# Two seams and a tail of a four-layer graph network: weights made one stage earlier, smaller loads, and a separate closing of the last run

## The chip, the cores and the metric

The kernel runs on one core of a Trainium2 chip. The metric is the device time of one execution in microseconds (us). Before the change three runs gave 1075.41, 1076.99 and 1079.09 us; the median is 1076.99.

The engines are TensorE (PE in the profile, with its weight loads as PEld), VectorE (DVE), ScalarE (ACT), GpSimd (POOL) and SyncE (SP), which here issues most transfers.

## The reference

The input is a table `x` of 2708 rows of 128 numbers and a 2708 x 2708 adjacency matrix `adj`, symmetric in its pattern, with about 17 non-zero weights in a row. Four layers follow each other. Each takes `h = relu(layernorm(x))`, and adds its result to `x`:

- layer 0: `adj.T @ h`, divided by the column sums of `adj`;
- layer 1: for each edge a message `gelu(s[i] + d[j] + b)`, summed with the edge's weight, then an update with a gelu and a layer norm;
- layer 2: `msg = relu((adj @ h) @ W_msg.T + b)`, then a GRU cell with `msg` as input and `h` as state;
- layer 3: graph attention with two heads `k`.

Layers 2 and 3 are the ones that the change touches. Layer 3 is, for each head:

```
z     = ln(h, g1, b1);           hk = z @ ff0_w[k].T
e     = leaky_relu(s_src[:, None] + s_dst[None, :])     # from hk and attn_w
atten = softmax(where(adj > 0 or i == j, e, -9e15))
att   = ln(atten @ hk + h, g2, b2)
result += elu(att @ ff1_w[k].T) / 2
```

## The kernel before, in words

**Tiles.** The 2708 rows are `NT` = 22 row tiles of 128 (the last has 20). Layer 0 leaves the transposed adjacency in HBM as `adjT`, tile by tile. Layers 0 and 1 end at about 621 us. The change begins there.

**Layer 2, groups.** The output columns are taken in six groups of four row tiles (512 columns; the last has two tiles, 148 columns). For each group, TensorE sums `h.T @ adjT` over all 22 row tiles into one accumulator, `p_agg` (L1088). The `adjT` tiles come in pieces of `PIECE` = 5 row tiles through a pool `a2` of three buffers; SP issues the load (L1076). Each piece is also turned into a byte mask "greater than zero" for layer 3: VectorE does all tiles but the last of a piece in one instruction (L1080), GpSimd the last (L1083). A buffer is free for the next load when both masks and TensorE's products are through.

**Layer 2, closing a group.** `finish_chunk` is a Python generator with the GRU of one group, and then what layer 3 needs of it: the norm of `x` to `h3`, a second norm to `z`, its transpose `p_z`, the product with the weights `p_hv`, and from that `hv` (the rows to be averaged), `lift` and `row` (exponentials of the scores). The generator yields with a number, and is resumed while the next group's products are written.

**Order of work.** Inside this stage the order of instructions is the order of the Python code. A hand-kept clock decides when a generator is resumed: every piece of TensorE work calls `spend(units)`, and `advance()` resumes each generator in `following` whose time has come. A unit is about one 512-column product. So `spend` and `yield` move no data; they place instructions in the queues. Each engine runs its queue in that order.

**Layer 3, runs.** Columns are taken in four runs, `RUNS` = tiles 0 to 2, 3 to 10, 11 to 18, 19 to 21. For each of 22 row tiles and 2 heads there is one unit: VectorE makes the weights `wt = max(row, lift) * mask` (L917), and TensorE multiplies them with `hv` into accumulators `att` (L949), one matmul per column tile. `products` makes weights a number `ahead` of the products: 2 for run 0, which still overlaps the closing of the last two groups of layer 2, and 3 for the others. Run 0 takes its weight buffers from a pool `l3v` of 4, the others from a pool of 5. A tile can be weighed when `finish_chunk` has put it in `ready`; `advance()` is called until it is.

**Closing a run.** When a run's products are done, `evacuate` copies its sums out of the accumulators, and `close` handles two tiles at a time while the next run's products go on: four rows `att_s` on VectorE (L1012), their statistics (L118 and L119, then L120), a power on GpSimd for the inverse deviation (L121) with one Newton step on VectorE (`factors`, L127 to L131), scaling on ScalarE (L137), transposes `p_aT` (L1023), `z4T` on ScalarE, the product `p_o` (L1032), the elu (`el`, `po` on ScalarE, `less` on GpSimd, `y` on VectorE, L1040 to L1050) and the store. `close_run` starts the closings `apart` = 9 units after each other. The last run has no following run; `in_place` lets `close` read the accumulators themselves, with 2 units between its two closings.

Of the kernel before, what the change touches and what calls it, by code (L numbers as in the profile page):

```python
# [20 lines left out]
F32 = mybir.dt.float32  # L21
BF16 = mybir.dt.bfloat16
AF = mybir.ActivationFunctionType
ALU = mybir.AluOpType
# [6 lines left out]
P = 128  # L31
N = 2708
D = 128
# [3 lines left out]
CH = 512  # L37
# [10 lines left out]
GROUPS = [(t, min(4, NT - t)) for t in range(0, NT, 4)]  # L48
# [3 lines left out]
def size(t):  # L52
    return min(P, N - t * P)
# [7 lines left out]
def listed_layers(ctx: ExitStack, tc: tile.TileContext, x, adj, w, out, flag):  # L61
    nc = tc.nc
# [10 lines left out]
    xs = const.tile([P, NT, D], F32, name="xs")  # L73
# [12 lines left out]
    ident = const.tile([P, P], F32, name="ident")  # L86
# [794 lines left out]
    nc.gpsimd.memset(score[:, NT - 1, :], 0.0)  # L881
    ident_8 = l3.tile([P, P], U8, name="ident_8")
    nc.vector.tensor_copy(ident_8, ident)
    PIECE = 5
    RUNS = ((0, 3), (3, 8), (11, 8), (19, 3))
    MOST = 8
    accs = ctx.enter_context(tc.tile_pool(name="l23p", bufs=1, space=PSUM))
# [5 lines left out]
    def follow(steps):  # L893
        following.append([steps, clock[0]])

    def spend(units):
        clock[0] += units

    def advance():

        for f in list(following):
            while f[1] <= clock[0]:
                wait = next(f[0], None)
                if wait is None:
                    following.remove(f)
                    break
                f[1] = clock[0] + wait

    ready = set()
# [10 lines left out]
        )  # L920
        return wt

    def products(run, numbers, pool, ahead, before=None):

        banks = None
        wts = []
        units = 2 * NT
        touched = set()
        for u in range(units + ahead):
            if u < units:  # L930
                while u // 2 not in ready:
                    spend(0.5)
                    advance()
                wts.append(weigh(run, u, pool))
            v = u - ahead
            if v < 0:
                continue
            if v == 0:
                if before:
                    before()  # L940
                banks = banks_of(run, numbers)
            r0, rn = run
            j, k = divmod(v, 2)
            kj = size(j)
            wt = wts[v]
            for q in range(rn):
                m = size(r0 + q)
                s = k * rn + q
                nc.tensor.matmul(  # L949
                    banks[s // 3][0:m, s % 3, :], wt[0:kj, q * P : q * P + m], hv[0:kj, j, k, :],  # L950
                    start=(v < 2 and s // 3 not in touched), stop=(j == NT - 1), skip_group_check=True,
                )
                touched.add(s // 3)
            spend(0.29 * rn)
            advance()
        return banks
# [4 lines left out]
            for b in numbers[0 : (2 * run[1] + 2) // 3]  # L961
        ]

    def in_place(run, banks):

        r0, rn = run
        sums = [banks[s // 3][:, s % 3, :] for s in range(2 * rn)]
        inv3 = out_pool.tile([P, 2 * MOST], F32, name="inv3")
        for k in range(2):
            for q0, q1 in ((0, rn - 1), (rn - 1, rn)):  # L970
                m, s = size(r0 + q1 - 1), k * rn
                if q1 > q0:
                    nc.vector.reciprocal(
                        inv3[0:m, s + q0 : s + q1], banks[s // 3][0:m, (s + q0) % 3 : (s + q1 - 1) % 3 + 1, D]
                    )
        return sums, inv3, False

    def evacuate(run, banks):

        r0, rn = run  # L980
        res = out_pool.tile([P, 2 * MOST, D + 1], F32, name="res")
        inv3 = out_pool.tile([P, 2 * MOST], F32, name="inv3")
        tails = (rn - 1, 2 * rn - 1) if size(r0 + rn - 1) < P else ()
        for s in tails:
            nc.gpsimd.memset(res[:, s, :], 1.0)
        s = 0
        while s < 2 * rn:
            k = min(3 - s % 3, 2 * rn - s)
            m = P
            if s in tails:  # L990
                k, m = 1, TAIL
            elif s + k - 1 in tails:
                k -= 1
            copy = nc.vector.tensor_copy if s // 3 % 3 == 2 else nc.scalar.copy
            copy(res[0:m, s : s + k, :], banks[s // 3][0:m, s % 3 : s % 3 + k, :])
            s += k
        nc.vector.reciprocal(inv3[:, 0 : 2 * rn], res[:, 0 : 2 * rn, D])
        return [res[:, s, :] for s in range(2 * rn)], inv3, True

    def close(run, sums, first):  # L1000

        res, inv3, whole = sums
        k0 = min(2, run[1] - first)
        t0 = run[0] + first
        n = 2 * k0
        att = out_pool.tile([P, 4, D], F32, name="att_s")
        for s in range(n):
            i = s % 2 * run[1] + first + s // 2
            m = P if whole else size(t0 + s // 2)
            if m < P:  # L1010
                nc.gpsimd.memset(att[:, s, :], 0.0)
            nc.vector.scalar_tensor_tensor(  # L1012
                att[0:m, s, :], res[i][0:m, 0:D], inv3[0:m, i : i + 1], h3[0:m, t0 + s // 2, :],
                op0=ALU.mult, op1=ALU.add,
            )
        rows = tiles_of(att, 0, n)
# [36 lines left out]
        for q in range(k0):  # L1053
            m, i = size(t0 + q), (t0 + q) * P
            nc.sync.dma_start(out[i : i + m, :], y[0:m, q, :])

    def close_run(run, sums, apart=9):

        for first in range(0, run[1], 2):
            follow(close(run, sums, first))  # L1060
            yield apart

    with (
        tc.tile_pool(name="l2a", bufs=3) as apool,
        tc.tile_pool(name="l2g", bufs=1) as pool,
        tc.tile_pool(name="l2z", bufs=2) as zpool,
        tc.tile_pool(name="l3v", bufs=4) as vpool,
        tc.manual_schedule(),
    ):
        def aggregate(t0, k0, pa, j0):  # L1070
# [23 lines left out]
        def finish_chunk(t0, k0, pa):  # L1094
# [23 lines left out]
            for k in range(2):  # L1118
                nc.tensor.matmul(prz[k][:, 0:n], W_hhT[:, k * D : (k + 1) * D], hc[:, 0:n], start=True, stop=False)

            gate = pool.tile([D, 2, CH], F32, name="gate")
            for k in range(2):
                nc.tensor.matmul(prz[k][:, 0:n], W_ihT[:, k * D : (k + 1) * D], msg[:, 0:n], start=False, stop=True)
                nc.scalar.activation(gate[:, k, 0:n], prz[k][:, 0:n], AF.Tanh, bias=gate_b[:, k : k + 1], scale=0.5)
            nc.tensor.matmul(pi[:, 0:n], W_ihT[:, 2 * D : 3 * D], msg[:, 0:n], start=True, stop=True)
            spend(7 * u)
            nn = pool.tile([D, CH], F32, tag="t2", name="nn")
            nc.vector.scalar_tensor_tensor(
                nn[:, 0:n], gate[:, 0, 0:n], 1.0, half_n[:, 0:n], op0=ALU.add, op1=ALU.mult
# [68 lines left out]
            for k in range(2):  # L1198
# [2 lines left out]
                    passed[k * k0 : (k + 1) * k0, :].rearrange("t i -> (t i)")[0:n].partition_broadcast(P),  # L1201
                )

        for g, (t0, k0) in enumerate(GROUPS):
            pa = accs.tile([P, CH], F32, tag=f"acc{g % 2}", name="p_agg")
            for j0 in range(0, NT, PIECE):
                aggregate(t0, k0, pa, j0)
            if t0 == 0:
                late_weights()
            follow(finish_chunk(t0, k0, pa))  # L1210
            advance()
        last = RUNS[0]
        banks = products(last, (0, 1), vpool, 2)

    out_pool = ctx.enter_context(tc.tile_pool(name="l3o", bufs=2))

# [8 lines left out]
    with tc.tile_pool(name="l3w", bufs=5) as wpool, tc.manual_schedule():  # L1225
        for run, numbers in zip(RUNS[1:], ((2, 3, 4, 5, 0, 1), (2, 3, 4, 5, 0, 1), (2, 3))):

            def work_off(last=last, banks=banks):
                follow(close_run(last, evacuate(last, banks)))

            banks = products(run, numbers, wpool, 3, work_off)
            last = run
        follow(close_run(last, in_place(last, banks), 2))
        while following:
            spend(1)
            advance()


@with_exitstack
# [459 lines left out]
```

## Time and profile before

The profiled execution took 1077.95 us, and its span is 1076.2 us.

| what | us |
|---|---|
| median of the runs | 1076.99 |
| profiled execution / its span | 1077.95 / 1076.2 |
| TensorE busy / VectorE busy | 950.2 (88%) / 824.4 (77%) |
| layer 2 aggregation, first matmul to last group's end | 627.4 to 781.9 |
| run 0, first matmul to last | 784.7 to 830.1 |
| run 3 ends, first reciprocal of its closing | 1053.7 |
| last `y` ready / span ends | 1070.4 / 1076.2 |

Engines are idle and busy together; a share over the whole span hides which stage is bound by what. A group's row gives what the group's instructions took together, the mean of one, and the idle time of the engine just before them with what ended it. A stretch's row gives busy us and number of instructions per engine, then the granted TensorE clock (1.00 is full), the share of the DMA engines and GB/s. A line of the waits gives us in total, number, and the longest. A timeline line gives start, length, engine, line and operation, and in brackets the idle time before it and what ended it.

### The profile page before, as it was taken

Reading aid. Unit: us, or ns where it says so; the run is one execution under the profiler, and the core shown is the slowest. Engines: PE = TensorE matmul, PEld = TensorE weight load, DVE = VectorE, ACT = ScalarE, POOL = GpSimd, SP = SyncE. Lnnn points to the kernel's source line nnn. Section 1 sums busy time; section 2 is a strip of 40 time slices with the busy share of each in tenths; the row PEclk is TensorE's granted clock in tenths of the full one; section 3 lists DMA queues with packets and bytes.
Section 4 is the critical chain, followed back from the end, with each engine's and each line's share of the span. In section 5 each row is a group of like instructions: output and inputs, shape, how many; then the busy total and the mean of one; then the engine's idle time right before and its main releaser. Section 6 shows DMA issues by size and latency. Waiting matters only on the chain. (4 is left out here: it accounts for less than half of the span.)

```text
span 1076.2 us, 21996 instructions
## 1 busy us (share of the span) xinstructions
PE 950.2 (88%) x7950; PEld 756.6 (70%) x7950; DVE 824.4 (77%) x2856; ACT 516.5 (48%) x1431; POOL 398.0 (37%) x476
## 2 busy tenths in 40 slices
PE   5798889854699999999999979999978999999993
PEld 2454455433599999899998934444578999999762
DVE  7999999658577888887878265666578977997673
ACT  7777778444666566666576522333321200320142
POOL 3311112013686556666765253434410300440132
PEclk9999999755799999999999979999989999999996
DMA  9888897221133333223222065666300000000000
GB/s 367 312 308 291 311 344 257 57 72 55 54 124 103 118 115 112 83 85 108 85 89 75 29 215 199 206 215 211 106 21 26 7 3 1 6 16 1 1 16 14
DMA packets 60625, 129.67 MB, mean 120 GB/s; under 512 B 11160, under 2 KB 23828, under 8 KB 57798
## 3 DMA queue, kind: packets, MB, share of 16 engines
q1 hardware_dynamic: 58690, 125.38, 33.7%
q10 hardware_dynamic: 1816, 2.80, 0.8%
q8 instruction: 64, 1.05, 0.4%
q14 instruction: 55, 0.45, 0.1%
HBM read 81.55 MB, written 30.87 MB: 104 GB/s over the span
## 5 line engine op out<-in xcount | busy, mean ns | idle before, releaser
L949 PE MATMUL att<-hv,wt 128*128 128x129 f32 (+2 forms) x1936 | 243.8, 283 | 8.8 <-DVE wt L917 8.8
L949 PEld LDWEIGHTS att<-hv,wt 128*128 128x128 f32 (+2 forms) x1936 | 224.7, 192 | 25.7 <-DVE wt L917 10.2
L917 DVE SCALAR_TENSOR_TENSOR wt<-row,lift,mask 128x1024 f32<-128x1024 f32 (+5 forms) x176 | 160.2, 939 | 35.1 <-PE att L949 35.1
L530 POOL TENSOR_SCALAR put<-mine,value 128x128 f32<-128x128 bf16 x176 | 149.6, 866 | 70.3 <-DVE mine L427 68.0
L606 PE MATMUL p_m<-s,sel 128*128 128x128 bf16 x1452 | 161.6, 220 | 5.4 <-ACT g L618 5.4
L610 PE MATMUL p_m<-d,cols 124*128 124x128 bf16 (+1 forms) x1452 | 161.8, 220 | 1.4 <-DVE cols L560 1.3
L121 POOL TENSOR_TENSOR n_r<-n_r,minus_half 128x4 f32<-128x4 f32 (+1 forms) x31 | 46.1, 1486 | 292.4 <-DVE n_r L120 286.8
L631 PE MATMUL agg<-put,g 128*128 128x128 f32 (+1 forms) x968 | 135.9, 281 | 0.0
L296 PE MATMUL acc<-a,hs 128*128 128x512 f32 (+2 forms) x264 | 119.8, 563 | 11.1 <-ACT hs L137 11.1
L308 PEld LDWEIGHTS p_T<-ident,a 128*128 128x128 f32 x484 | 61.3, 147 | 85.7 <-issue 38.4
L631 PEld LDWEIGHTS agg<-put,g 128*128 128x128 f32 x968 | 118.2, 192 | 0.0
L1088 PE MATMUL p_agg<-a,hs 128*128 128x512 f32 (+2 forms) x264 | 109.4, 557 | 7.5 <-DMA a<-adjT 7.5
L606 PEld LDWEIGHTS <-sel 128*128 128x128 bf16 x1452 | 104.3, 98 | 10.8 <-issue 7.0
L308 PE MATMUL p_T<-ident,a 128*128 128x128 f32 x484 | 84.3, 295 | 30.9 <-ACT aT L312 23.5
L284 DVE FIND_INDEX8 col<-val,a 128x8 uint16<-128x124 f32 (+1 forms) x400 | 109.2, 290 | 0.0
L610 PEld LDWEIGHTS <-cols 124*128 124x128 bf16 (+1 forms) x1452 | 102.6, 98 | 1.9 <-DVE cols L560 1.9
L618 ACT ACTIVATE g<-p_m 128x512 f32<-128x512 f32 x132 | 73.0, 553 | 63.5 <-PE p_m L610 63.5
L538 ACT ACTIVATE put<-mine,value 128x128 f32<-128x128 bf16 x308 | 100.5, 391 | 0.0
L312 ACT ACTIVATE aT<-p_T 128x512 f32<-128x512 f32 (+2 forms) x132 | 71.1, 541 | 52.8 <-ACT aT L312 27.6
L282 DVE MAX8 val<-a 128x8 f32<-128x124 f32 (+1 forms) x400 | 94.2, 282 | 2.1 <-DMA a<-in_adj 2.1
L1088 PEld LDWEIGHTS p_agg<-a,hs 128*128 128x128 f32 (+1 forms) x264 | 47.6, 194 | 55.9 <-issue 54.3
L296 PEld LDWEIGHTS acc<-a,hs 128*128 128x128 f32 (+1 forms) x264 | 44.6, 199 | 31.2 <-issue 19.9
(249 smaller groups left out, 1423.7 us busy)
## 6 DMA issues: line engine op xcount, KB each, us to landing
a<-in_adj SPq DMA_DIRECT2D x21, 1354.0 KB
adjT<-aT SPq DMA_DIRECT2D x105, 256.0 KB
a<-adjT SPq DMA_DIRECT2D x20, 1280.0 KB
spread<-passed SPq DMA_DIRECT2D x22, 704.0 KB
later<-sel SPq DMA_DIRECT2D x22, 616.0 KB
row<-own_d ACTq DMA_DIRECT2D x10, 256.0 KB
later<-sel SPq DMA_DIRECT2D x22, 82.5 KB
adjT<-aT SPq DMA_DIRECT2D x21, 74.0 KB
```

What stands on the lines that cost most here:

```text
L282: nc.vector.max(val[:, n, b, :], block(b))
L284: nc.vector.max_index(col[:, n, b, :], val[:, n, b, :], block(b))
L296: nc.tensor.matmul(accs[ci][:, 0:cw], h[0:m, n, :], sets[n // 4][0:m, n % 4, c : c + cw], start=(n == 0), stop=(n == NT - 1),)
L308: nc.tensor.transpose(p[0:k, q * P : q * P + m], sets[gi][0:m, q, j * P : j * P + k], ident[0:m, 0:m])
L530: nc.gpsimd.tensor_scalar(st["put", 0][:, b, :], st["mine"][:, b, :], st["value"][:, b : b + 1], None, ALU.mult)
L538: nc.scalar.activation(st["put", 1][:, b - HP, :], st["mine"][:, b, :], AF.Identity, scale=st["value"][:, b : b + 1])
L606: nc.tensor.matmul(p[:, b - b0, :], st["sel"][:, b, :], s3[:, q, t % 2, :], start=(q == 0), stop=False)
L610: nc.tensor.matmul(p[:, b - b0, :], st["cols"][0:kb, b, :], d3[0:kb, b, q, :], start=False, stop=(q == 2))
L631: nc.tensor.matmul(agg, g[:, b - 4 * k, :], put, start=(b == 0), stop=False)
L917: nc.vector.scalar_tensor_tensor(wt[0:kj, :], row[0:kj, k, c : c + n], lift[0:kj, j, k : k + 1], mask[0:kj, j, c : c + n], op0=ALU.max, op ...
L949: nc.tensor.matmul(banks[s // 3][0:m, s % 3, :], wt[0:kj, q * P : q * P + m], hv[0:kj, j, k, :], start=(v < 2 and s // 3 not in touched), ...
L1088: nc.tensor.matmul(pa[:, 0:n], h[0:k, j, :], a[0:k, j - j0, 0:n], start=(j == 0), stop=(j == NT - 1))
```

## The change

Four things change, all in layers 2 and 3.

1. Pieces have four row tiles instead of five: six loads per group (4, 4, 4, 4, 4, 2), and the `a2` buffers shrink by a fifth. The pool `l3v` grows from 4 to 8 buffers.
2. While group 4 is aggregated, `weigh_ahead` makes two weights of run 0 after each piece but the first, up to seven, where their tiles are ready. `products` gets them as `made`, and works run 0 with 7 ahead. For the last, small group `finish_chunk` spends and yields once more between its gate matmuls.
3. The closings of run 2 start 7 units apart instead of 9.
4. The last run is closed by `close_last`, straight-line code in place of two resumed generators: both parts' statistics first, rows scaled alternately on ScalarE and VectorE, `z4T` of the second part and `po` on VectorE, and `less` and the clearing of short rows done beforehand by `last_rows`. `in_place` goes, and with it the flag `whole`.

```diff
--- before.py
+++ after.py
@@ -881,7 +881,7 @@
     nc.gpsimd.memset(score[:, NT - 1, :], 0.0)
     ident_8 = l3.tile([P, P], U8, name="ident_8")
     nc.vector.tensor_copy(ident_8, ident)
-    PIECE = 5
+    PIECE = 4
     RUNS = ((0, 3), (3, 8), (11, 8), (19, 3))
     MOST = 8
     accs = ctx.enter_context(tc.tile_pool(name="l23p", bufs=1, space=PSUM))
@@ -920,14 +920,20 @@
         )
         return wt
 
-    def products(run, numbers, pool, ahead, before=None):
+    def weigh_ahead(run, wts, pool, most):
+
+        for u in range(len(wts), min(len(wts) + 2, most)):
+            if u // 2 in ready:
+                wts.append(weigh(run, u, pool))
+
+    def products(run, numbers, pool, ahead, before=None, made=()):
 
         banks = None
-        wts = []
+        wts = list(made)
         units = 2 * NT
         touched = set()
         for u in range(units + ahead):
-            if u < units:
+            if len(wts) <= u < units:
                 while u // 2 not in ready:
                     spend(0.5)
                     advance()
@@ -961,20 +967,6 @@
             for b in numbers[0 : (2 * run[1] + 2) // 3]
         ]
 
-    def in_place(run, banks):
...
     def evacuate(run, banks):
 
         r0, rn = run
@@ -995,22 +987,19 @@
             copy(res[0:m, s : s + k, :], banks[s // 3][0:m, s % 3 : s % 3 + k, :])
             s += k
         nc.vector.reciprocal(inv3[:, 0 : 2 * rn], res[:, 0 : 2 * rn, D])
-        return [res[:, s, :] for s in range(2 * rn)], inv3, True
+        return [res[:, s, :] for s in range(2 * rn)], inv3
 
     def close(run, sums, first):
 
-        res, inv3, whole = sums
+        res, inv3 = sums
         k0 = min(2, run[1] - first)
         t0 = run[0] + first
         n = 2 * k0
         att = out_pool.tile([P, 4, D], F32, name="att_s")
         for s in range(n):
             i = s % 2 * run[1] + first + s // 2
-            m = P if whole else size(t0 + s // 2)
-            if m < P:
-                nc.gpsimd.memset(att[:, s, :], 0.0)
             nc.vector.scalar_tensor_tensor(
-                att[0:m, s, :], res[i][0:m, 0:D], inv3[0:m, i : i + 1], h3[0:m, t0 + s // 2, :],
+                att[:, s, :], res[i][:, 0:D], inv3[:, i : i + 1], h3[:, t0 + s // 2, :],
                 op0=ALU.mult, op1=ALU.add,
             )
         rows = tiles_of(att, 0, n)
@@ -1054,6 +1043,82 @@
             m, i = size(t0 + q), (t0 + q) * P
             nc.sync.dma_start(out[i : i + m, :], y[0:m, q, :])
 
+    def last_rows(run):
+
+        res = out_pool.tile([P, 2 * MOST, D + 1], F32, name="res")
+        rn = run[1]
+        nc.gpsimd.memset(res[:, 2 * rn - 2 : 2 * rn, :], 0.0)
+        less = out_pool.tile([P, 2 * MOST, D + 1], F32, name="res")[:, 0:rn, 0:D]
+        nc.gpsimd.tensor_scalar(less, xs[:, run[0] : run[0] + rn, :], -1.0, None, ALU.add)
+        return res[:, 0 : 2 * rn, 0:D], less
+
+    def close_last(run, banks, att, less):
+
+        r0, rn = run
+        inv3 = out_pool.tile([P, 2 * MOST], F32, name="inv3")
+        parts = ((0, rn - 1), (rn - 1, rn))
+        mvs = []
+        for q0, q1 in parts:
+            m = size(r0 + q1 - 1)
+            for k in range(2):
+                nc.vector.reciprocal(inv3[0:m, k * rn + q0 : k * rn + q1], banks[k][0:m, q0:q1, D])
+            for q in range(q0, q1):
+                for k in range(2):
+                    nc.vector.scalar_tensor_tensor(
+                        att[0:m, 2 * q + k, :], banks[k][0:m, q, 0:D], inv3[0:m, k * rn + q : k * rn + q + 1],
+                        h3[0:m, r0 + q, :], op0=ALU.mult, op1=ALU.add,
+                    )
+            mvs.append(moments(tiles_of(att, 2 * q0, 2 * (q1 - q0)), f"n{5 + q0}"))
+        turned, sums = [], []
+        for (q0, q1), (mv, r) in zip(parts, mvs):
+            rstd, shift = factors(mv, r)
+            n = 2 * (q1 - q0)
+            p = bank("p_aT")
+            for s in range(n):
+                rows = att[:, 2 * q0 + s, :]
+                if s % 2:
+                    nc.vector.tensor_scalar(
+                        rows, rows, rstd[:, s : s + 1], shift[:, s : s + 1], ALU.mult, ALU.add
+                    )
+                else:
+                    nc.scalar.activation(
+                        rows, rows, AF.Identity, bias=shift[:, s : s + 1], scale=rstd[:, s : s + 1]
+                    )
+            for s in range(n):
+                nc.tensor.transpose(p[:, s * P : (s + 1) * P], att[:, 2 * q0 + s, :], ident)
+            zT = out_pool.tile([P, 4, P], F32, name="z4T")[:, 0:n, :]
+            pv = p.rearrange("p (s i) -> p s i", s=4)[:, 0:n, :]
+            if q0 == 0:
+                nc.scalar.activation(zT, pv, AF.Identity, bias=shift2, scale=gain2)
+            else:
+                nc.vector.tensor_scalar(zT, pv, gain2, shift2, ALU.mult, ALU.add)
+            turned.append(zT)
+        for (q0, q1), zT in zip(parts, turned):
+            p = bank("p_o")
+            for s in range(2 * (q1 - q0)):
+                nc.tensor.matmul(
+                    p[:, s * D : (s + 1) * D], zT[:, s, :], ff1T[:, s % 2 * D : (s % 2 + 1) * D], start=True, stop=True
+                )
+            sums.append(p.rearrange("p (q k d) -> p q k d", q=2, k=2)[:, 0 : q1 - q0, :, :])
+        els, pos = [], []
+        for (q0, q1), v in zip(parts, sums):
+            els.append(out_pool.tile([P, 2, 2, D], F32, name="el")[:, 0 : q1 - q0, :, :])
+            pos.append(out_pool.tile([P, 2, 2, D], F32, name="po")[:, 0 : q1 - q0, :, :])
+            nc.scalar.activation(els[-1], v, AF.Relu, scale=-1.0)
+            nc.scalar.activation(els[-1], els[-1], AF.Exp, scale=-1.0)
+            nc.vector.tensor_scalar(pos[-1], v, 0.0, 0.5, ALU.max, ALU.mult)
+            nc.vector.tensor_tensor(pos[-1][:, :, 0, :], pos[-1][:, :, 0, :], pos[-1][:, :, 1, :], ALU.add)
+            nc.gpsimd.tensor_tensor(less[:, q0:q1, :], less[:, q0:q1, :], pos[-1][:, :, 0, :], ALU.add)
+        for (q0, q1), el in zip(parts, els):
+            y = out_pool.tile([P, 2, D], F32, name="y")
+            nc.vector.tensor_tensor(el[:, :, 0, :], el[:, :, 0, :], el[:, :, 1, :], ALU.add)
+            nc.vector.scalar_tensor_tensor(
+                y[:, 0 : q1 - q0, :], el[:, :, 0, :], 0.5, less[:, q0:q1, :], op0=ALU.mult, op1=ALU.add
+            )
+            for q in range(q0, q1):
+                m, i = size(r0 + q), (r0 + q) * P
+                nc.sync.dma_start(out[i : i + m, :], y[0:m, q - q0, :])
+
     def close_run(run, sums, apart=9):
 
         for first in range(0, run[1], 2):
@@ -1064,7 +1129,7 @@
         tc.tile_pool(name="l2a", bufs=3) as apool,
         tc.tile_pool(name="l2g", bufs=1) as pool,
         tc.tile_pool(name="l2z", bufs=2) as zpool,
-        tc.tile_pool(name="l3v", bufs=4) as vpool,
+        tc.tile_pool(name="l3v", bufs=8) as vpool,
         tc.manual_schedule(),
     ):
         def aggregate(t0, k0, pa, j0):
@@ -1118,12 +1183,15 @@
             for k in range(2):
                 nc.tensor.matmul(prz[k][:, 0:n], W_hhT[:, k * D : (k + 1) * D], hc[:, 0:n], start=True, stop=False)
 
+            if n < CH:
+                spend(4 * u)
+                yield 0.5
             gate = pool.tile([D, 2, CH], F32, name="gate")
             for k in range(2):
                 nc.tensor.matmul(prz[k][:, 0:n], W_ihT[:, k * D : (k + 1) * D], msg[:, 0:n], start=False, stop=True)
                 nc.scalar.activation(gate[:, k, 0:n], prz[k][:, 0:n], AF.Tanh, bias=gate_b[:, k : k + 1], scale=0.5)
             nc.tensor.matmul(pi[:, 0:n], W_ihT[:, 2 * D : 3 * D], msg[:, 0:n], start=True, stop=True)
-            spend(7 * u)
+            spend(7 * u if n == CH else 3 * u)
             nn = pool.tile([D, CH], F32, tag="t2", name="nn")
             nc.vector.scalar_tensor_tensor(
                 nn[:, 0:n], gate[:, 0, 0:n], 1.0, half_n[:, 0:n], op0=ALU.add, op1=ALU.mult
@@ -1201,16 +1269,19 @@
                     passed[k * k0 : (k + 1) * k0, :].rearrange("t i -> (t i)")[0:n].partition_broadcast(P),
                 )
 
+        last = RUNS[0]
+        made = []
         for g, (t0, k0) in enumerate(GROUPS):
             pa = accs.tile([P, CH], F32, tag=f"acc{g % 2}", name="p_agg")
             for j0 in range(0, NT, PIECE):
                 aggregate(t0, k0, pa, j0)
+                if g + 2 == len(GROUPS) and j0 >= PIECE:
+                    weigh_ahead(last, made, vpool, 7)
             if t0 == 0:
                 late_weights()
             follow(finish_chunk(t0, k0, pa))
             advance()
-        last = RUNS[0]
-        banks = products(last, (0, 1), vpool, 2)
+        banks = products(last, (0, 1), vpool, 7, None, made)
 
     out_pool = ctx.enter_context(tc.tile_pool(name="l3o", bufs=2))
 
@@ -1225,15 +1296,16 @@
     with tc.tile_pool(name="l3w", bufs=5) as wpool, tc.manual_schedule():
         for run, numbers in zip(RUNS[1:], ((2, 3, 4, 5, 0, 1), (2, 3, 4, 5, 0, 1), (2, 3))):
 
-            def work_off(last=last, banks=banks):
-                follow(close_run(last, evacuate(last, banks)))
+            def work_off(last=last, banks=banks, apart=7 if run == RUNS[-1] else 9):
+                follow(close_run(last, evacuate(last, banks), apart))
 
             banks = products(run, numbers, wpool, 3, work_off)
             last = run
-        follow(close_run(last, in_place(last, banks), 2))
+        att, less = last_rows(last)
         while following:
             spend(1)
             advance()
+        close_last(last, banks, att, less)
 
 
 @with_exitstack
```

More of the change, by code (lines that the diff above doesn't have):

```diff
@@ L962, in banks_of @@
         ]
-    def in_place(run, banks):
[L966 to L976, printed above, removed]
     def evacuate(run, banks):
```

## The prediction

> **What bounds the kernel now.** I read the profiled execution by stages first, then what TensorE waited for, then single tiles. The profiled execution took 1077.95 us (span 1076.2, 1.75 us around it); the median of the runs shown is 1076.99, about 1 us less. My sum is made against the profiled execution and its difference is taken from the median.
>
> The table of stretches (bounds in us, then busy us and count per engine, granted clock, DMA share, GB/s), cut to the stretches that count:
>
> ```profile
> 620.00:627.40 7.40, 1.35 (x6) 0.54 (x6) 5.04 (x24) 3.72 (x10) 1.79 (x2) 0.50 0.66 229
> 633.20:652.00 18.80, 17.74 (x47) 7.83 (x46) 12.25 (x33) 3.59 (x9) 14.76 (x10) 1.00 0.57 189
> 652.00:752.00 100.00, 98.44 (x269) 46.06 (x268) 61.92 (x162) 35.12 (x96) 38.14 (x22) 1.00 0.59 202
> 784.70:790.10 5.40, 5.36 (x23) 5.39 (x24) 1.48 (x3) 0.77 (x2) 0.78 (x1) 0.50 0.00 0
> 790.10:830.20 40.10, 35.42 (x279) 32.14 (x277) 33.79 (x102) 10.36 (x41) 3.02 (x3) 1.00 0.08 28
> 1004.00:1053.60 49.60, 49.60 (x316) 34.24 (x314) 36.23 (x122) 16.35 (x33) 15.52 (x16) 0.97 0.03 9
> ```
>
> TensorE (first number) is full in layer 2 (652 to 752) and in run 3 (1004 to 1053.6). It is not full at the start of layer 2, in run 0 (784.7 to 830.2, with half clock at first), and in the tail after 1053.6. The waits of the first and second of these places:
>
> ```profile
> PE p_agg L1088 <- DMA a<-adjT: 7.0, 2, 6.1
> ...
> PE att L949 <- DVE wt L917: 8.8, 9, 2.7
> ```
>
> The first row is group 0 (6.1 us for the first load, 0.87 for the fourth); the second is run 0, where TensorE waits nine times for VectorE's weights. For the masks that free the load buffers, and the chain of the tail, instruction by instruction (start, us):
>
> ```profile
> L1083 POOL TENSOR_SCALAR mask<-a x6: 1482/1970/3177, 635.9 to 649.1; 128x512 uint8<-128x512 f32 x5, 20x512 uint8<-20x512 f32 x1
> L1080 DVE TENSOR_SCALAR mask<-a x5: 819/1215/1634, 636.8 to 646.7; 128x2048 uint8<-128x2048 f32 x4, 128x512 uint8<-128x512 f32 x1
> ```
> ```profile
> 1056.63 0.42 DVE L1049 TENSOR_TENSOR el<-el 128x256 f32<-128x256 f32 x1
> 1058.13 0.60 DVE L1012 SCALAR_TENSOR_TENSOR att_s<-att,inv,h 20x128 f32<-20x128 f32 x2 [0.56 <-POOL att_s L1011]
> 1060.66 2.42 ACT L137 ACTIVATE att_s<-att_s,n_r 128x128 f32<-128x128 f32 x6 [9.06 <-DVE n_r L131]
> 1063.80 2.93 PE L1032 MATMUL p_o<-ff1T,z4T 128*128 128x128 f32 x12 [0.19 <-ACT z4T L1026]
> 1070.14 0.29 DVE L1050 SCALAR_TENSOR_TENSOR y<-el,less 128x128 f32<-128x128 f32 x1 [0.41 <-POOL less L1046]
> ```
>
> No mask of layer 2 starts before 635.9, because POOL and DVE finish layer 1 first; so group 0 runs on what its buffers hold. In the tail no engine is full: it is a chain.
>
> [...] (half clock 783.3 to 790.1 and 831.1 to 834.5, 6.8 and 3.4 us) [...] gaps of 2.74 and 1.43 us were enough, one of 0.87 was not. [...] the fourth load issues at 638.50, when POOL's first mask ends at 638.46, and lands at 644.24. [...] here a POOL mask took 1.48 us at least and up to 3.18 beside DVE.
>
> **Part 1, pieces of four.** Three buffers hold 12 tiles, not 15. A load is 1.05 MB, not 1.31; at about 395 GB/s that is 0.66 us less, so TensorE starts at some 626.6 instead of 627.43. The fourth load still waits for the first masks: POOL's one tile is the same 2.5 us from 635.9; DVE has three tiles (about 0.94 us by the ratio of 1.22 for four). It issues at about 638.3 and needs 5.74 - 0.66 = 5.1 us: 643.3. TensorE has used its 12 tiles by about 640.4 (3.8 at half clock until 633.2, the rest at 0.88 us). So it idles 2.9 us where it idled 0.87. Ten tiles are left: 643.3 + 10 x 0.88 = 652.1, against 650.7: +1.4. If the clock drops for one window (3.4 us at half), 1.7 more: +3.1. By the gaps above a drop is likely: I take +2.8, ends +1.4 and +3.6. Layer 2 is then TensorE-bound (98.44 of 100), so nothing gives this back.
> The sixth load per group is one more SP issue of 0.37 us; SP has over 20 us per group for six: nothing, unless the load is late. The one wait of 0.6 us on a load in 652 to 752 shows that the slack is small; +0.2, ends -0.3 and +0.8. POOL masks six full or part tiles per group instead of five, about 1.7 us each, with 38 of 100 us busy: nothing of itself, but the power step of a norm queues behind a mask, included below.
>
> **Part 2, weights ahead.** Seven 128x384 weights, 0.55 us apart on DVE, go into group 4, two after a piece. DVE is 18 of 29 us busy there, so 3.85 us fit as work; but it is in order, and two of them plus a mask stand ahead of the norms of the earlier group, whose z feeds TensorE's p_z. There DVE waited for POOL 0.9 twice and for h 0.6, and TensorE waited 0.83 us for z at 765.5. Two weights are 1.1 us: +1.1, ends +0.3 and +1.8. The extra memory (four buffers of 384 floats, 6 KB a partition) is what the load buffers give up.
> At the transition, TensorE now has seven units when group 5's products end, instead of waiting from 781.95 to 784.74. Before, run 0 idled 8.8 us up to 831.5 (7.4 of them before 830.1), and had half clock to 790.1. I laid DVE's new order out with the old durations: y at 790.7, the statistics of x 792.2 to 794.0, four weights to 796.2, the last factors 799.1, z on ACT 799.2 to 800.9. TensorE has used its weights by about 798.7 and waits for z until 801.2, say 2 us net. Run 0 then ends at 824.9 if the clock stays, 826.6 if that wait drops it, against 830.1: -5.2 or -3.5. I take -4.2. The new yield of 0.5 and the spends of 4u and 3u in the last group (u is 148/512) only place a unit between gate matmuls; what they cost is in that layout. The 1.43 us gap to run 1 stays, since its first weight still waits for TensorE's last matmul of run 0.
>
> **Part 3, closings of run 2 seven apart.** In run 3 a closing costs DVE 1.1 (rows) + 1.8 (statistics) + 0.9 (factors) + 0.9 (sum and y) = 4.6 us by the rows of that stretch. Seven units of the hand clock are about 5.4 units of weights at 0.5: 2.7. DVE needs 7.3 us per closing, TensorE about 6.9. DVE lags about 0.4 us four times, 1.6 us, against a lead of three units, 2.9 us, of which one block of 2.85 us (rows and statistics) takes nearly all. Before (nine apart) there was no stall. +0.8, ends 0 and +3.
>
> **Part 4, close_last.** Gone from DVE's chain: the last sum and y of run 2 (0.95) and the wait for a memset (0.56, now made ahead); two reciprocals more (0.3). Factors start about 1.1 us earlier. Rows go two and two to ACT and DVE (before six on ACT, 2.42), but TensorE still turns the second part before the first p_o: p_o starts about 1 us earlier (9.1 against 10.13 after the first reciprocal). Then `po` moves from ACT to DVE, `less` is ready, and POOL has one operation per part instead of three: relu, exp, `po`, `less`, y end 14.9 to 15.3 against 16.76. I take -1.7, ends -0.7 and -2.5.
>
> **Sum.** +2.8 + 0.2 + 1.1 - 4.2 + 0.8 - 1.7 = -1.0 us, so the profiled execution would be 1077.0 and the median **1076.0**. Two gains of together 5.9 are met by losses of 4.9.
>
> **Rivals.**
> Bounds of the measurement: 0.3% is 3.2 us, about what the runs (1075.4 to 1079.1) can tell.
> *A, forecast:* within 3.2 us of before, 44 in 100, own range 1074 to 1079.
> *B, the gains stay and the losses don't:* no clock drop in group 0 (+1.4), z of group 4 only 0.4 late, no drop at p_z (-5.2), run 3 keeps its lead (0), tail -2.0: -5.4, 1071.6. For it: [...] DVE has 11 us free in group 4. [...] 28 in 100.
> *C, slower: DVE becomes the bound of run 3.* Place: the four closings of run 2. Price: if the block of 2.85 us finds the lead already used, each of three closings stalls TensorE 1 to 2 us, and such a gap halves the clock for a window (1.7): about +6 instead of +0.8, 1081.2. It decides from 5 us of stall in run 3. For it: DVE's 107% by the sum above. Against: the average before is only 36.23 busy of 49.6, so DVE catches up at both ends. 17 in 100.
> *D, the weights ahead only move the wait:* DVE still has the same total before the last z and the last scores; TensorE runs through its seven units and waits at p_z for what it saved, the clock drops, and run 0 ends only 1 us earlier: -1.0 instead of -4.2, 1079.2, and with a worse group 0 1080.5. For it: 33.79 of 40.1 us busy on DVE. Against: seven weights (3.85 us) did leave this stretch. 11 in 100, at the edge between same and slower.
>
> **Range.** 80% needs A, most of B and of D, so 1071.2 to 1081.0; the far ends (tail and transition both at their best, or C in full) are left out. Faster than 1073.8: B, 0.28. Slower than 1080.2: C and most of D, 0.17 + 0.08 = 0.25. The rest 0.47.
>
> **What would show it.** Group 0: TensorE's wait for a load is about 2.9 us at 640 to 643 (right), and the granted clock after it 0.5 for a window; a wait under 1 us proves me wrong. Weights ahead: rows of `wt` in group 4, no gap at the start of run 0, a wait for z of 2 us or more inside it, last matmul of run 0 about 4 us earlier relative to the transposes p_h of group 5. Run 3: TensorE's wait on `wt` after closings; none in B, over 5 us in C. Tail: last y 15 us after the first reciprocal of the last run. If the gap at run 0 to run 1 vanishes or TensorE stalls between groups, my reading of the queues was wrong.

## The result, and the profile after

The changed kernel takes as long as the one before: 1077.55 us (median of four runs, 1076.10 to 1079.48) against 1077.44 (1075.41 to 1079.09), a ratio of 1.0003 with a 95% interval of 0.9979 to 1.0027. Its profiled execution has a span of 1075.9 us. That nothing moved is the sum of moves of up to seven us in both directions.

The table of stretches of the changed kernel, cut at the places that count (columns as before: bounds, then busy us and count per engine, granted clock, DMA share, GB/s):

```profile
619.40:624.90 5.50, 0.00 (x0) 0.02 (x1) 3.83 (x21) 2.31 (x6) 1.31 (x2) 0.50 0.82 275
...
638.10:641.80 3.70, 0.00 (x0) 0.02 (x1) 2.69 (x9) 0.88 (x2) 0.99 (x3) 0.82 0.97 355
641.80:654.20 12.40, 12.26 (x24) 5.17 (x24) 5.07 (x11) 0.59 (x1) 5.29 (x4) 0.78 0.59 197
...
770.00:777.00 7.00, 4.83 (x19) 3.86 (x19) 3.69 (x13) 3.40 (x7) 3.95 (x5) 0.76 0.34 87
...
807.40:811.00 3.60, 3.54 (x15) 2.94 (x16) 3.46 (x11) 2.59 (x6) 0.00 (x0) 0.54 0.01 2
811.00:832.30 21.30, 21.23 (x169) 19.65 (x168) 15.73 (x45) 4.44 (x27) 0.91 (x1) 1.00 0.08 26
...
1004.00:1053.30 49.30, 49.30 (x316) 34.33 (x315) 36.65 (x123) 16.77 (x34) 17.38 (x18) 0.97 0.04 12
```

Group 0 has a hole of 3.7 us and a lowered clock after it. A second hole, with lowered clock, lies at 770 to 777, where before TensorE was busy throughout. Run 0 is full from 811 to its end, and run 3 (1004 to 1053) is full as before. TensorE's waits between 619 and 835:

```profile
PE p_agg L1153 <- DMA a<-adjT: 5.9, 2, 5.6
PE p_z L155 <- ACT z L137: 4.3, 2, 2.3
PE p_agg L1153 <- ACT hs L137: 3.7, 1, 3.7
PE att L955 <- ACT res L987: 1.4, 1, 1.4
PE p_row L1260 <- DVE hv L1247: 1.4, 2, 0.7
```

The row of weights, 8.8 us before, is gone. New are two waits for z at p_z (2.0 at the end of group 4, 2.3 in run 0) and two of 0.7 for `hv`. The third row is the hole in group 0. The profile names ScalarE's last norm (it ends at 641.75), but the first mask of the fourth load waits for that load until 641.70: the two end together. The masks, by tile (minimum/median/maximum in ns), in the first 35 us of the stage:

```profile
L1148 POOL TENSOR_SCALAR mask<-a x7: 1477/1487/1507, 633.9 to 653.3; 128x512 uint8<-128x512 f32 x6, 20x512 uint8<-20x512 f32 x1
L1145 DVE TENSOR_SCALAR mask<-a x6: 715/1736/1753, 634.8 to 646.7; 128x1536 uint8<-128x1536 f32 x5, 128x512 uint8<-128x512 f32 x1
```

Here is what I had not expected. VectorE's mask of three tiles takes 1.74 us; the mask of four took 1.22. And GpSimd's are steady at 1.49 where they went up to 3.2 beside the old ones. What this does ahead of z in group 4, in order of time:

```profile
767.67 1.14 DVE L917 SCALAR_TENSOR_TENSOR wt<-row,lift,mask 128x384 f32<-128x384 f32 x2
...
768.73 1.75 DVE L1145 TENSOR_SCALAR mask<-a 128x1536 uint8<-128x1536 f32 x1
...
770.39 0.15 DVE L127 TENSOR_TENSOR n3z_r<-n3z_r 128x4 f32<-128x4 f32 x1
...
772.30 1.59 PE L155 MATMUL p_z<-ident,z 128*128 128x128 f32 x4 [1.99 <-ACT z L137]
```

Two weights and a slow mask stand in VectorE's queue ahead of the factors, which start at 770.39; TensorE waits. The tail:

```profile
1054.31 0.17 DVE L1064 RECIPROCAL inv<-att 128x2 f32<-128x2 f32 x1 [0.79 <-PE att L955]
...
1060.00 0.88 ACT L1084 ACTIVATE res<-res,n_r 128x128 f32<-128x128 f32 x2 [11.63 <-DVE n_r L131]
...
1063.40 2.77 PE L1099 MATMUL p_o<-ff1T,z4T 128*128 128x128 f32 x12
...
1069.32 0.29 DVE L1115 SCALAR_TENSOR_TENSOR y<-el,res 128x128 f32<-128x128 f32 x1
```

The last y ends 15.3 us after this reciprocal; it was 16.8.

### The profile page after: what moved, and what is told of

Read it like the earlier page. It is cut to its first block, busy times and chain, and to the rows that moved or that the text cites. A ratio compares the mean times of both kernels' runs of the same rounds, so it can differ in the third digit from the quotient of the medians.

```text
span 1075.9 us, 22019 instructions
## 1 busy us (share of the span) xinstructions
PE 949.4 (88%) x7950; PEld 755.2 (70%) x7950; DVE 840.0 (78%) x2870; ACT 516.1 (48%) x1425; POOL 391.5 (36%) x478
## 5 line engine op out<-in xcount | busy, mean ns | idle before, releaser
L955 PE MATMUL att<-hv,wt 128*128 128x129 f32 (+2 forms) x1936 | 240.4, 281 | 1.4 <-ACT res L987 1.4
L121 POOL TENSOR_TENSOR n_r<-n_r,minus_half 128x4 f32<-128x4 f32 (+1 forms) x31 | 42.7, 1376 | 284.8 <-DVE n_r L120 273.4
L1153 PE MATMUL p_agg<-a,hs 128*128 128x512 f32 (+2 forms) x264 | 113.3, 572 | 9.7 <-DMA a<-adjT 5.9
L284 DVE FIND_INDEX8 col<-val,a 128x8 uint16<-128x124 f32 (+1 forms) x400 | 113.9, 314 | 0.0
L282 DVE MAX8 val<-a 128x8 f32<-128x124 f32 (+1 forms) x400 | 98.9, 306 | 2.3 <-DMA a<-in_adj 2.3
```

Of the source, the lines that this page charges most:

```text
L282: nc.vector.max(val[:, n, b, :], block(b))
L284: nc.vector.max_index(col[:, n, b, :], val[:, n, b, :], block(b))
L955: nc.tensor.matmul(banks[s // 3][0:m, s % 3, :], wt[0:kj, q * P : q * P + m], hv[0:kj, j, k, :], start=(v < 2 and s // 3 not in touched), ...
L1153: nc.tensor.matmul(pa[:, 0:n], h[0:k, j, :], a[0:k, j - j0, 0:n], start=(j == 0), stop=(j == NT - 1))
```

## The experiments

**How they are compared.** Each ratio is to runs of the kernel before on the same chip; e8 and e9 ran on another chip than the other experiments. Beside it I cut each profile into stages, by instructions that all kernels have: A, from the last product of layer 1 (`p_u`) to the transposes `p_h` of group 0; B, from there to the `p_h` of group 5; C, from there to run 1's first matmul; D, from there to the last run's reciprocal of all full tiles; E, from there to the end of the last y. All in us; "l1" is where layer 1's products ended.

| kernel | l1 | A | B | C | D | E | ratio, 95% interval |
|---|---|---|---|---|---|---|---|
| before | 621.4 | 30.1 | 130.1 | 50.0 | 222.1 | 16.8 | 1 |
| before, second profile | 617.7 | 32.4 | 130.1 | 49.0 | 222.1 | 16.8 | one run, 1075.81 us |
| changed | 619.3 | 34.9 | 136.7 | 42.7 | 220.6 | 15.3 | 1.0003, 0.9979 to 1.0027 |
| e1 pieces only | 618.8 | 35.2 | 132.1 | 48.8 | 221.9 | 16.8 | 1.0036, 1.0014 to 1.0057 |
| e2 all masks on VectorE | 618.7 | 33.1 | 131.8 | 43.1 | 220.5 | 15.3 | 0.9955, 0.9943 to 0.9967 |
| e3 no weights ahead | 619.0 | 35.0 | 132.3 | 48.9 | 219.0 | 15.7 | 1.0029, 1.0014 to 1.0044 |
| e4 old tail | 618.9 | 34.6 | 136.4 | 42.7 | 220.6 | 16.8 | 1.0019, 1.0008 to 1.0029 |
| e6 masks, other axis order | 617.9 | 33.9 | 132.7 | 42.8 | 220.6 | 15.3 | 0.9967, 0.9951 to 0.9982 |
| e7 pieces of two | 621.2 | 29.2 | 132.2 | 43.0 | 220.5 | 15.3 | 0.9916, 0.9893 to 0.9939 |
| e8 as e2, no weights ahead | 617.0 | 34.8 | 130.9 | 49.4 | 222.2 | 15.7 | 1.0012, 0.9999 to 1.0026 |
| e9 closings nine apart | 618.6 | 35.4 | 136.6 | 42.7 | 220.6 | 15.5 | one run, 1077.16 us |

The theories. P: the pieces of four cost what layer 2 lost, through a dry spell in group 0 and slow masks. W: the weights made ahead cost it, through z.

**e1, pieces of four alone.**

Against the kernel before:

```diff
-    PIECE = 5
+    PIECE = 4
```

> The kernel before with pieces of four alone. Theory P (in the changed kernel the pieces cost most of what layer 2 lost: group 0 runs dry after 12 tiles and the clock halves, and a mask of three tiles takes VectorE 1.74 us where one of four took 1.22): group 0 ends 4 to 5 us later after the end of layer 1, group 5's p_h 5 to 7 us later, nothing elsewhere, so 1.005 to 1.007 of before. Theory W (the weights made ahead cost the most): group 5's p_h at most 3 us later, ratio under 1.003.

Measured: 1.0036. A is 3.9 longer than the mean of the two profiles of before (31.2), B 2.0: together 5.9 us up to group 5's `p_h`, as P said (7.1 against the first profile of before, 4.8 against the second, both nearer to P than to W). The ratio is worth 3.9 us and below P's 1.005, though its interval reaches it. The pieces cost, but of the 6.6 us that B lost in the changed kernel they explain 2.0 only.

**e3, no weights ahead.**

Against the changed kernel:

```diff
-                if g + 2 == len(GROUPS) and j0 >= PIECE:
+                if False:
                     weigh_ahead(last, made, vpool, 7)
...
-        banks = products(last, (0, 1), vpool, 7, None, made)
+        banks = products(last, (0, 1), vpool, 2, None, made)
```

> The changed kernel with no weights in group 4 and run 0 two ahead, as before. Theory P: group 5's p_h comes 3 to 5 us earlier than in the changed kernel (the wait for z at p_z falls from 2.0 to about 0.8, without a halved clock), and run 0 takes its old 48.6 us from p_h to its last matmul instead of 41.3: 2 to 4 us slower than the changed kernel, ratio 1.002 to 1.004. Theory W: group 5's p_h comes 8 us or more earlier and the kernel is as fast as the changed one or faster, ratio 1.000 or below.

Measured: 1.0029; B falls by 4.4 and C grows by 6.1. In run 0 TensorE waits for weights again, as in the kernel before:

```profile
PE att L955 <- DVE wt L917: 7.0, 8, 2.2
PE p_row L1260 <- DVE hv L1247: 1.4, 2, 0.7
```

So the weights ahead gain, as P said, but they pay 4.4 us for 6.1: 1.7 net in these two stages, 2.8 by the ratios (0.0026), whose intervals allow both, and just no gain at all; e8 is the clearer case. The two waits of 0.7 stay, and e1 has them too: they belong to the pieces. e1 is without the new yield between the gate matmuls and e3 has it, and their B and C agree within 0.2 us: the yield alone moves nothing.

**e2, all masks on VectorE.**

Against the changed kernel:

```diff
-            most = min(whole, PIECE - 1)
+            most = whole
```

> The changed kernel, but VectorE masks all four tiles of a piece in one instruction and GpSimd only the short last tile. If the odd count of three tiles is what makes the mask slow, this one takes 1.22 us or less (more elements in less time), TensorE's waits at p_row (0.7 twice) go, the wait at p_z of group 4 falls from 2.0 to under 1 and the clock stays there: 3 to 5 us less than the changed kernel, ratio to before 0.996 to 0.998. If the form of the mask is covered by other work anyway, the ratio stays within 0.001 of the changed kernel's 1.000; if the mask's cost is by element, it takes 2.3 us and the kernel gets slower.

Measured: 0.9955, which is 5.2 us less than the changed kernel's ratio, a little more than expected. VectorE now masks a third more elements in less time. Its row of the groups by shape (busy us, mean ns, idle before it):

```profile
L1145 DVE TENSOR_SCALAR mask<-a 128x2048 uint8<-128x2048 f32 x25 | 30.3, 1219 | 5.1 <-DMA a<-adjT 5.1
```

It was 43.4 us, 1743 ns, in the changed kernel. And TensorE's waits from 652 to 835:

```profile
PE p_z L155 <- ACT z L137: 2.7, 2, 2.3
...
PE p_row L1260 <- DVE hv L1247: 0.3, 2, 0.2
```

The wait at the p_z at the end of group 4 fell from 2.0 to 0.35, those at `p_row` from 0.7 each to 0.16; B fell by 4.9 us. But this edit also takes 25 full masks away from GpSimd, so it can't tell the form of VectorE's mask from GpSimd's share. e6 can.

**e6, the same three tiles in another order.**

Against the changed kernel:

```diff
-            nc.vector.tensor_scalar(mask[:, j0 : j0 + most, c : c + n], a[:, 0:most, 0:n], 0.0, None, ALU.is_gt)
+            halves = "p t (b i) -> p b t i"
+            nc.vector.tensor_scalar(
+                mask[:, j0 : j0 + most, c : c + n].rearrange(halves, b=2), a[:, 0:most, 0:n].rearrange(halves, b=2),
+                0.0, None, ALU.is_gt,
+            )
```

> The changed kernel, with the same three tiles per mask on VectorE, the same one on GpSimd, the same elements: only the order of the axes of the instruction is another, two half rows outermost in place of three tiles. If an odd outermost count is what makes the mask slow, it takes about 0.95 us (three quarters of 1.22) instead of 1.74, GpSimd's masks go up from 1.49 to 2 us or more beside it, and the kernel comes to 0.996 to 0.998. If it is the number of elements or the output type, the mask stays at 1.74 and the ratio at 1.000.

Measured: 0.9967, within the 0.996 to 0.998 expected for an odd count, and these groups by shape:

```profile
L1152 POOL TENSOR_SCALAR mask<-a 128x512 uint8<-128x512 f32 x25 | 43.5, 1746 | 12.0 <-DMA a<-adjT 12.0
L1146 DVE TENSOR_SCALAR mask<-a 128x1536 uint8<-128x1536 f32 x25 | 25.4, 1024 | 0.7 <-DMA a<-adjT 0.6
```

The same elements, types and engine take 1.02 us in place of 1.74 when two half rows, and not three tiles, are the outermost count; GpSimd's masks go up from 1.49 to 1.75 beside them, less than the 2 that I expected. So the order of the axes makes the mask slow, and not the number of elements or the output type.

Is it enough that the count is odd? The last group has rows of 148 and answers that. Its masks of three tiles in the changed kernel and of four in e2, from the groups by shape:

```profile
L1145 DVE TENSOR_SCALAR mask<-a 128x444 uint8<-128x444 f32 x5 | 2.4, 478 | 0.0
```
```profile
L1145 DVE TENSOR_SCALAR mask<-a 128x592 uint8<-128x592 f32 x5 | 2.4, 481 | 0.0
```

Three rows of 148 take as long as four, no longer. The patterns that the trace records for the two masks of three tiles differ. A row of 512 fills its row of the buffer, so three rows follow each other without a gap, and the slow mask reads one run of 1536 and writes three rows of 512. In the last group it reads three rows of 148 and writes three. In e6, by its edit, both counts are two. Of these forms the slow mask alone has an odd count at the destination that the source doesn't share. Three rows of 512 on both sides were not run.

**e8, masks of four tiles without weights ahead.** The edit is e2's and e3's together.

> The kernel with all four masks on VectorE, without the weights in group 4 and with run 0 two ahead as before. With slow masks the weights ahead gained 0.0026 of the time (1.0029 without, 1.0003 with), since they cost 4.4 us between the p_h of group 0 and that of group 5 and gave back 6.1 in run 0. If the 4.4 us come from slow masks and weights meeting on VectorE ahead of z, they cost under 1 us here and gain 5 to 6 us: this kernel then stands 5 to 6 us above 0.9955, at 1.000 to 1.002. If weights cost z the same whatever the masks do, it stands at 0.997 to 0.998.

Measured: 1.0012, as the first reading said. With e2, e3 and the changed kernel it makes a square. With masks of 1.74 us the weights ahead cost B 4.4 us (132.3 to 136.7); with masks of 1.22 us 0.9 (130.9 to 131.8). In C they gain 6.1 and 6.3. That is one profile each, but B repeats within 0.3 us where the same layer 2 was profiled again (before 130.1 twice; changed, e4 and e9 136.4 to 136.7). In ratios they are worth 0.0026 with the longer masks and 0.0057 with the shorter; the difference of the two, 0.0031, is no larger than its interval. Neither P nor W was whole: of the 6.6 us that B lost, some 3.5 (4.4 less 0.9) are the two meeting in VectorE's queue.

**e4 and e9, the tail.** e4 has the old closing with closings nine apart; e9 only this line:

Against the changed kernel:

```diff
-            def work_off(last=last, banks=banks, apart=7 if run == RUNS[-1] else 9):
+            def work_off(last=last, banks=banks, apart=9):
```

> The changed kernel with the old closing of the last run and closings of run 2 nine apart. By the two traces the last y comes 15.3 us after the last run's first reciprocal of all sums with the new routine and 16.8 with the old, and run 3 does not stall with either distance: 1.5 us slower than the changed kernel, ratio 1.0015. If closings seven apart did cost run 3 something, the difference is smaller, down to 0.

> The changed kernel with closings of run 2 nine apart again and the new closing of the last run. Seven apart is worth the last sum and y of run 2, which then end inside run 3: here they stand between the statistics of the two last parts, and the last y comes 0.9 us later after the reciprocal, at 16.2 us instead of 15.3; run 3 takes the same time with either. If the new routine alone makes the tail short, it stays at 15.3.

e4 measured 1.0019, 0.0016 above the changed kernel as expected, though inside the intervals; E is 16.8 again and D is the same 220.6. In e9 my first reading failed: E is 15.5, not 16.2. VectorE in order of time:

```profile
1052.96 0.43 DVE L1039 SCALAR_TENSOR_TENSOR y<-el,less 128x256 f32<-128x256 f32 x1 [0.61 <-POOL less L1035]
...
1053.84 0.17 DVE L1064 RECIPROCAL inv<-att 128x2 f32<-128x2 f32 x1 [0.37 <-PE att L955]
...
1069.00 0.29 DVE L1115 SCALAR_TENSOR_TENSOR y<-el,res 128x128 f32<-128x128 f32 x1
```

The last y of run 2 now fits in before VectorE waits for TensorE's last sums, since the new routine starts only when the older closings have run out. So the routine makes the tail short. Seven apart costs run 3 nothing, and what it adds can't be told: the 0.15 us between 15.45 here and 15.30 is less than the 0.4 by which E differs in e3 and e8 (15.7), which have the changed kernel's closing.

**e7, pieces of two.**

Against the kernel of e2:

```diff
-    PIECE = 4
+    PIECE = 2
-        tc.tile_pool(name="l2a", bufs=3) as apool,
+        tc.tile_pool(name="l2a", bufs=6) as apool,
-                if g + 2 == len(GROUPS) and j0 >= PIECE:
+                if g + 2 == len(GROUPS) and j0 >= 6 and j0 % 4 == 2:
```

> The kernel of the masks on VectorE (0.9955 of before), with pieces of two tiles in six buffers: the same 24 KB and the same 12 tiles ahead, but a buffer comes free after two tiles are masked. If group 0's dry spell comes from the grain of the loads, the first load lands 1 us or more earlier, the idle time of 2.5 us at the 13th tile falls under 0.7 and the halved clock after it goes: 3 to 5 us less, ratio 0.991 to 0.993. If the first masks' start after layer 1 and the load's latency are what count, the gap shrinks by 1 us at most, and with 11 loads and 11 masks per group the ratio stays at 0.995 to 0.997.

Measured: 0.9916, 1068.07 us, faster than both kernels. But only half of my reason held. TensorE's two waits in group 0, from its timeline:

```profile
625.62 4.55 PE L1153 MATMUL p_agg<-a,hs 128*128 128x512 f32 x6 [4.46 <-DMA a<-adjT]
...
640.62 9.02 PE L1153 MATMUL p_agg<-a,hs 128*128 128x512 f32 x20 [2.73 <-DMA a<-adjT]
```

The first load does land 1.1 us earlier after layer 1 (4.46 against 5.53 in e2). The hole at the 13th tile stays at 2.7, where I expected under 0.7; it was 2.5 in e2. The 3.9 us by which A is shorter than in e2 come from the first load (1.1), a clock that was full earlier in the first 12 tiles (12.3 against 13.5 us) and no halved clock after the hole (1.7). How much of the clock is the grain of the loads, and how much differs from one execution to the next, one profile can't say; the ratio over all runs of e7 (0.0039 below e2) suggests that most of it recurs, though the two intervals leave anything from 1.4 to 7 us.

**e5, the kernel before again.**

> The kernel before, unchanged, for a second profile. In its first profile layer 1 ended 2.0 us later than in the changed kernel's, and 2.3 to 2.6 us later than in the first three experiments with pieces of four, though layers 0 and 1 have the same code. If that is the spread from one execution to the next, layer 1 ends here at 619 or anywhere within 2 us of it; if the changed kernels really reach layer 2 earlier, it ends at about 621.3 again.

Layer 1 ended at 617.7, 3.6 us earlier than in the first profile of the same code: it is the spread between executions. Group 0 differed as well. From its timeline:

```profile
641.37 8.01 PE L1088 MATMUL p_agg<-a,hs 128*128 128x512 f32 x14 [2.67 <-DMA a<-adjT]
```

The hole that was 0.87 us in the first profile is 2.67 here, since TensorE ran at half clock only until about 627.5, 9.8 us after layer 1 and not 11.9, and was through with its 15 tiles sooner. The profile on which I predicted was a lucky one for this stage by 2.3 us.

## Why the prediction was right, and where it was not

The forecast (1076.0, no change that can be told) and its range held, but by luck: errors of several us in both directions met. In order of the sum, against the mean of the two profiles of before:

- **Group 0, +2.8 (1.4 to 3.6): measured +3.7** (4.9 against the first profile, 2.6 against the second). The restart was forecast at 643.3 and came at 643.8 on the clock of before (641.81 + 2.03, the distance of the two ends of layer 1). Two errors cancel in that: GpSimd's first mask ended 1.0 us earlier than forecast (635.4, which is 637.4 on the clock of before), but the fourth load then waited for VectorE's first mask instead, which ended at 636.51, and was issued at 636.65 (638.7, forecast 638.3). TensorE's start, 626.6, should by the forecast's own 0.66 have been 626.8; it was 626.9. The mis-sized term is the clock: half for 6.8 us (640.4 to 647.3), not for 3.4.
- **The mask of three tiles, "about 0.94 us by the ratio of 1.22 for four": measured 1.74.** This is the step that failed. I scaled by elements a duration that depends on the order of the axes too: the same elements took 1.02 us in e6. "GpSimd's one tile is the same 2.5 us" failed with it: 1.49.
- **Weights ahead before z, +1.1, and loads, +0.2: measured +6.6 over B.** The pieces alone cost 2.0 there (e1), the weights 4.4 on top (e3). The mechanism was named (two weights and a mask ahead of the norms), its size was not: the mask was 0.8 longer than I took it for, the wait became 2.0 long, and the clock then stood at half for 3.4 us (773.6 to 777.0). I also read the 0.83 us of the old p_z as a wait; it was the length of its four transposes, which take 0.60 where nothing holds them up.
- **Run 0, -4.2 (-5.2 to -3.5): measured -6.8** (-7.3 against the first profile, from which it was forecast). The wait for z inside it was forecast at 2 and is 2.3, with the halved clock that I allowed for. The two stretches below, before and changed, run from the `p_h` of group 5 to run 0's last product. TensorE's idle time fell from 7.3 to 2.4 us: 4.9, near the forecast 5.4 (7.4 less 2). And the same 301 products took 2.4 us less, with the clock at half for 3.4 us in place of 6.8. Part 2 names the half clock at the start of run 0 and charges the new one with 1.7, but gives the loss of the old one no worth: that is the mis-sized step. Against the second profile, which has 3.4 us of half clock in this stretch too, the products are still 1.4 us shorter; why, isn't shown. z started on ScalarE at 797.3 on the clock of before (806.80, less the 9.46 us between the two `p_h` of group 5), not at 799.2. The last gate products came 3.5 us after `p_h` and not 7.9; 2.8 of this is the wait for weights that is gone, the rest goes with the full clock.
- **Run 3, +0.8: measured 0.** TensorE is busy 49.30 of 49.30 us. VectorE's lag of 107% never became a wait. Rival C falls.
- **The tail, -1.7: measured -1.5.** Its steps came nearly as laid out: the factors 1.3 us earlier (forecast 1.1), p_o 9.1 us after the reciprocal (9.1), the end at 15.3 (14.9 to 15.3). That the last sum and y of run 2 leave the chain by the new routine stands in Part 4 and is right; it was only before e9 that I put it down to seven apart.
- **Not foreseen: -1.5 in D.** The half clock in runs 1 to 3 lasted 10.2 us and not 13.7, which is 1.7 us at half speed. e3, with 219.0, and e8, with 222.2, show that it follows no edit; what sets it isn't shown.

The stretches of run 0, before and changed:

```profile
781.51:829.77 48.26, 40.94 (x301) 37.66 (x302) 38.26 (x118) 11.35 (x44) 4.54 (x4) 0.93 0.07 23
```
```profile
790.97:831.95 40.98, 38.54 (x301) 36.20 (x302) 33.90 (x110) 11.30 (x44) 4.54 (x4) 0.96 0.08 27
```

The measured terms add up to +0.5 us (3.7 + 6.6 - 6.8 - 1.5 - 1.5), beside 0.3 by the ratio. Rival D (the weights only move the wait) falls by stage C; rival B got its gain in run 0, but none of its small losses.

Where the prediction says a window it counts 3.4 us, the shortest half clock of its trace (831.1 to 834.5). That a hole drops the clock was my estimate, from two gaps of that one trace. In the changed kernel half clock came with the holes of 3.7, 2.0 and 2.3 us: from 640.4 to 647.3, 773.6 to 777.0 and 807.7 to 811.1. A wait of 0.35 at the p_z of group 4 (e2) had none behind it. In e7 one of 2.73 had none either (20 products in 9.02 us, 11.72 in the changed kernel), and in e6 a wait of 0.56 at the same p_z was followed by half speed (the four transposes p_h at 767.1 took 0.98 us, 0.60 in e2), though the prediction read 0.87 as too short. The gap of 1.4 us between runs 0 and 1 was followed by half clock in the changed kernel (835.0 to 838.4) and not in e2, whose 96 products after it took 10.96 us and not 12.60. So the length of a hole alone doesn't decide, and what does isn't shown.

## What to carry to other kernels

Don't scale a VectorE duration by the number of elements alone: when a tile count changes, look at how the instruction's patterns change with it (here from one run of 2048 written as four rows, 1.22 us, to one of 1536 written as three, 1.74), time the new form, and try another order of the axes (1.02 us for the same elements). Two edits that each add a little to one in-order queue ahead of the same wait are not worth the sum of their single effects (the weights ahead cost B 4.4 us beside masks of 1.74 us and 0.9 beside masks of 1.22); cost what stands ahead of the critical instruction together. And compare by stages between marks that both kernels have: the same code before the change spread over 4.4 us (617.0 to 621.4) in these profiles, as much as the larger edits moved.

## What the runs showed of the hardware

- A VectorE comparison from 128x1536 float to bytes takes 1.74 us when it reads one run of 1536 and writes three rows of 512 (changed kernel), and 1.02 us as two by three rows of 256 (e6); 128x2048, read as one run and written as four rows, takes 1.22 us (e2), and 128x1024, written as two, 0.69 (e7). With three rows read and three written in the last group, 128x444 takes 0.48 us (changed kernel), as long as 128x592 with four tiles (e2). Why the first form is the slow one isn't shown.
- GpSimd's 128x512 mask takes 1.49 us on average beside VectorE masks of 1.74 us (changed kernel), and 1.75 beside those of 1.22 (before) and 1.02 us (e6). What makes it longer there isn't shown.
